# Cross attention in fp32: seven block products for two more batches, softmax sums taken by ScalarE, and the last tile's product in two column halves

## The chip, the core and the metric

The kernel runs on one core of a Trainium2 chip. The core has TensorE (matrix products, named PE in the profile, with its weight loads as PEld), VectorE (DVE), ScalarE (ACT), GpSimd (POOL) and SyncE (SP), which here issues the transfers between HBM and the on-chip memory (SBUF). TensorE writes its products into PSUM, eight banks that VectorE and ScalarE empty. Every engine works through its own queue in order, and waits at semaphores for the others. The metric is the device time of one execution in microseconds (us); less is better.

## The reference

There are 16 batches of 256 rows of x with 256 columns, and for each batch a context c of 77 rows with 192 columns. Eight heads of width 256 attend from x to c; the result is projected, added to x and normalised:

```python
Q = (x @ Wq).reshape(B, 256, 8, 256)        # and K, V from c with Wk, Wv
score = einsum('bhqd,bhkd->bhqk', Q, K) / sqrt(256)     # -inf where the mask is 0
attn = softmax(score)
out = einsum('bhqk,bhkd->bqhd', attn, V).reshape(B, 256, 2048) @ Wo + x
out = (out - mean(out)) * rsqrt(var(out) + 1e-5) * gamma + beta     # over the 256 columns
```

Everything is fp32. The output has 16 x 256 x 256 numbers.

## The kernel before

**Weights first.** For about 54 us the kernel multiplies the weights with each other: per head it forms Wq Wk^T (`gA`, `gB`) and Wv Wo (`uA`, `uB`). Afterwards the projections of x and of the output are gone: scores are x times `a`, where `a` = (Wq Wk^T) c^T, and the output is the softmax weights times `vw`, where `vw` = c (Wv Wo).

**The main loop.** It starts at line 862 and runs over batches, with b from -1 to 14. An iteration works on three batches: `new` is batch b + 1 (scores and softmax), `now` is batch b (product of the softmax weights with `vw`), `old` is batch b - 1 (layer norm and store). A batch is two tiles of 128 rows; tiles 2b and 2b + 1 belong to batch b. Each engine's instructions stand in the order in which the code issues them (`manual_schedule`), so the order of the calls is the order of the queues.

TensorE's part of an iteration: `scores` for both new tiles (line 319, into two PSUM banks for each tile), `prepare_vw` (lines 244 and 255), for b up to 10 also one quarter of `a` for the next group of four batches (`prepare_a`, lines 202 and 216), and then the product for batch b. For batches 0 to 10 (b < NS = 11) that is `seven`: the product of a batch is seen as a two by two block product, and seven block products are formed where eight would be the plain number. It needs `differences` of `vw` (`ts`, on GpSimd, line 398) and `sums` of the transposed weights (`ss`, GpSimd, lines 415 to 418), both for the next batch at the end of an iteration, and afterwards `add_seven`: ScalarE copies `m` out of PSUM (line 458), VectorE adds `po` to the rows of x (line 482), and GpSimd adds `m` (line 468, two adds in `m` and three to x). For batches 11 to 15 it is `attend` for each tile (line 384): the plain product, 256 columns wide, and one add on VectorE.

The softmax of a tile: `shift` on VectorE adds the mask from PSUM (line 334, twice) and takes the maximum (line 341); `exponential` on ScalarE, one instruction for each of eight heads (line 348); `weigh` sums each head on VectorE (line 354), takes the reciprocal (line 356) and multiplies on GpSimd (line 362, two pieces); `turn` transposes 32 by 32 blocks on VectorE (line 372) for TensorE.

The layer norm of a tile: `finish` takes statistics on VectorE (lines 490 and 493), `spread` forms the reciprocal root on ScalarE with a logarithm and an exponential (lines 502 and 503), `normalise` is either two VectorE instructions (lines 523 and 539) or, with `aside`, one on ScalarE (line 533) and two on GpSimd (lines 534 and 535), after a small scalar `less` (line 513). The stores are issued by SP, two tiles at a time (line 546), and the last two tiles one at a time (line 956).

After the loop the last batch is multiplied with `attend` for tiles 30 and 31, the layer norm of tiles 28 and 29 is done with `aside`, and those of tiles 30 and 31 follow one after the other on VectorE.

The PSUM ring has eight banks (`ps_mm`), given out in the order of the calls.

Of the kernel before, what the change touches and what calls it, by code (L numbers as in the profile page):

```python
# [8 lines left out]
F32 = mybir.dt.float32  # L9
I32 = mybir.dt.int32  # L10
AF = mybir.ActivationFunctionType
ALU = mybir.AluOpType
AX = mybir.AxisListType
PSUM = bass.MemoryType.PSUM

P = 128
H = 8
D = 256
EPS = 1e-05
GB = 4  # L20
# [33 lines left out]
def kernel(  # L54
# [53 lines left out]
    NH = DI // 2 // BK  # L108
    uA = const.tile([P, 5, NH, NF, BK], F32, tag="uA", name="uA")
    uB = const.tile([P, 5, NH, NF, BK], F32, tag="uB", name="uB")  # L110
    NS = B - GB - 1

    def of_e(u, e):
        return u[:, 3 - 2 * e : 5 - 2 * e].rearrange("p q n i c -> p (q n) i c")
# [226 lines left out]
        nc.vector.tensor_reduce(top, s, AX.X, ALU.max, negate=True)  # L341
        s_of[t] = s, top

    def exponential(t):
        e = sp.tile([P, H, S2], F32, tag="e", name=f"e_{t}")
        s, top = s_of.pop(t)
        for h in range(H):
            nc.scalar.activation(e[:, h], s[:, h], AF.Exp, bias=top[:, h : h + 1])  # L348
        e_of[t] = e

    def weigh(t):
        e = e_of.pop(t)
        den = st.tile([P, H], F32, tag="den", name=f"den_{t}")
        nc.vector.tensor_reduce(den, e, AX.X, ALU.add)  # L354
        rden = st.tile([P, H], F32, tag="rden", name=f"rden_{t}")
        nc.vector.reciprocal(rden, den)  # L356
        p = p_ring[t % 2]
        e_mh = e.rearrange("p (m h) k -> p m h k", h=2)
        rden_mh = rden.rearrange("p (m h) -> p m h", h=2)
        for cols, keys in ((slice(2 * KM), slice(KM)), (slice(2 * KM, 2 * S2), slice(KM, None))):  # L360
            part = p[:, :, cols].rearrange("p m (h k) -> p m h k", h=2)
            nc.gpsimd.tensor_tensor(  # L362
                part,
                e_mh[:, :, :, keys],
                rden_mh.unsqueeze(3).to_broadcast(list(part.shape)),
                ALU.mult,
            )
# [11 lines left out]
    def attend(t):  # L379
# [10 lines left out]
                )  # L390
        po_of[t] = po


    def differences(b):

        vw = vw_of[b].rearrange("p q k d -> p q (k d)")
        ts = vwp.tile([P, 3, 2, P], F32, tag="ts", name=f"ts_{b}", bufs=2)
        nc.gpsimd.tensor_tensor(  # L398
            ts.rearrange("p q k d -> p q (k d)"),
            vw[:, 1:4],  # L400
            vw[:, 0:1].to_broadcast([P, 3, 2 * P]),
            ALU.subtract,
        )
        ts_of[b] = ts
# [16 lines left out]
    def seven(b):  # L421
        pT = [pT_of.pop(QT * b + i) for i in range(QT)]
        vw, ss = vw_of[b], ss_of.pop(b)
        ts = ts_of.pop(b)
        pm = ps_mm.tile([P, 4, P], F32, tag="mm", name=f"pm_{b}")
        po = ps_mm.tile([P, 4, P], F32, tag="mm", name=f"po_{b}")
        t2, b21, b22, b11 = (vw[:, q] for q in range(4))
        t4, t1, t3 = (ts[:, q] for q in range(3))
        s1, s3, s2, s4 = (ss[:, i] for i in range(4))
        ends = vr[:, b, :P], vr[:, b, P:]  # L430

        def contract(out, *terms):
            for n, (weight, moving) in enumerate(terms):
                for i in range(NM):
                    nc.tensor.matmul(  # L435
                        out[i * BK : (i + 1) * BK],
                        weight[:, i],
                        moving,
                        start=(n == 0),
                        stop=(n == len(terms) - 1),  # L440
                    )

        def block(weights, moving):
            return [(weights[:, k], moving[:, k]) for k in range(2)]

        last = [(pT[i][:, NF], vr[:, b, j * P : (j + 1) * P]) for i in range(QT) for j in range(2)]
        contract(pm[:, 0], *block(pT[0][:, 0:2], b11))
        contract(pm[:, 1], *block(s2, t2))
        contract(pm[:, 2], *block(s3, t3))
        contract(pm[:, 3], *block(s1, t1))  # L450
        contract(po[:, 0], *block(pT[0][:, 2:4], b21), last[0])
        contract(po[:, 1], *block(s4, b22), last[1])
        contract(po[:, 2], *block(pT[1][:, 2:4], t4), last[2])
        contract(po[:, 3], last[3])
        for i in range(QT):
            po_of[QT * b + i] = flat(po[:, 2 * i : 2 * i + 2])
        m = vwp.tile([P, 4, P], F32, tag="m", name=f"m_{b}", bufs=1)
        nc.scalar.copy(m, pm)
        m_of[b] = m
# [24 lines left out]
    def finish(t):  # L484
        if t in po_of:
            add_product(t)
        g, j = t // GT, t % GT
        y = xg_of[g][:, j, :]
        bn = st.tile([P, 6], F32, tag="bn", name=f"bn_{t}")
        nc.vector.bn_stats(bn, y)  # L490
        if j == 0:
            mv_of[g] = st.tile([P, GT, 2], F32, tag="mv", name=f"mv_{g}", bufs=2)
        nc.vector.bn_aggr(mv_of[g][:, j, :], bn)

    all_rstd_of, rstd_of, done = {}, {}, []

    def spread(first, last):

        g, lo, hi = first // GT, first % GT, (last - 1) % GT + 1
        log = st.tile([P, GT], F32, tag="log", name=f"log_{first}")  # L500
        rstd = st.tile([P, GT], F32, tag="rstd", name=f"rstd_{first}")
        nc.scalar.activation(log[:, lo:hi], mv_of[g][:, lo:hi, 1], AF.Ln, bias=eps)
        nc.scalar.activation(rstd[:, lo:hi], log[:, lo:hi], AF.Exp, scale=-0.5)
        all_rstd_of[first, last] = rstd
# [16 lines left out]
    def centre(t):  # L521
        y = xg_of[t // GT][:, t % GT, :]
        nc.vector.scalar_tensor_tensor(
            y, y, mv_of[t // GT][:, t % GT, 0:1], gam, ALU.subtract, ALU.mult
        )
# [336 lines left out]
    for b in range(-1, B - 1):  # L862
        old = range(max(b - 1, 0) * QT, b * QT)
        now = range(max(b, 0) * QT, (b + 1) * QT)
        new = range((b + 1) * QT, (b + 2) * QT)
        for t in new:
            scores(t)
        if b == B - 2:
            for t in old:
                finish(t)  # L870
            spread(old[0], old[-1] + 1)
            invert(old[0], old[-1] + 1, aside=old)
            for t in old:
                normalise(t, aside=True)
        for t in new:
            shift(t)
        for n in range(0, 2) if b < 0 else range(b + 2, min(b + 3, B // 2)):
            turn_last(n)
        g, n = (b + 1) // GB + 1, (b + 1) % GB
        work = [prepare_vw(b + 1)]  # L880
        if g < NG:
            work.append(prepare_a(g, (n,)))
        for part_A, _, _ in work:
            part_A()
        for _, part_B, _ in work:
            part_B()
        for i, t in enumerate(new):
            exponential(t)
            if old and b < B - 2:
                finish(old[i])  # L890
            weigh(t)
        if old and b < B - 2:
            spread(old[0], old[-1] + 1)
        for _, _, copies in work:
            for dst, src in copies():
                nc.scalar.copy(dst, src)  # L896
        if b + 1 < NS:
            differences(b + 1)
        if b < NS:
            if now:  # L900
                seven(b)
            if old:
                invert(old[0], old[-1] + 1)
                normalise(old[0])
            for t in new:
                turn(t)
            if n >= NF - 2:
                for j in range((n - NF + 2) * GT // 2, (n - NF + 3) * GT // 2, 2):
                    transpose_x(g, j)
            if old:  # L910
                normalise(old[1])


            if n == NF - 1:
                load_x(g)
            elif n:
                load_xT(g, (n - 1) * GT // 2, n * GT // 2)
            if now:
                add_seven(b)
            if b + 1 < NS:  # L920
                sums(b + 1)
            continue
        for t in now:
            attend(t)
        if b < B - 2:
            invert(old[0], old[-1] + 1, aside=old[:1])
            normalise(old[0], aside=True)
            turn(new[0])
            normalise(old[1])
            turn(new[1])  # L930
            for t in now:
                add_product(t)
        else:
            turn(new[0])
            finish(now[0])
            spread(now[0], now[1])
            turn(new[1])

    for t in new:
        attend(t)
    add_product(last - 2)
    for t in (last - 3, last - 2):
        invert(t, t + 1, aside=(t,), less_on=nc.vector)
        normalise(t, aside=True)
        if t < last - 2:
            finish(t + 1)
            spread(t + 1, t + 2)
    for t in (last - 1, last):  # L950
        finish(t)
        spread(t, t + 1)
        centre(t)
        invert(t, t + 1)
        normalise(t, centred=True)
        nc.sync.dma_start(out_rows[:, t, :], xg_of[NG - 1][:, t % GT, :])


# [29 lines left out]
```

## Time and profile before

| what | value |
|---|---|
| median of 3 runs (lowest, highest) | 277.38 us (276.35, 278.02) |
| the profiled execution's own time | 276.75 us |
| its span | 274.9 us |
| TensorE busy | 267.8 us, 97% of the span |
| VectorE busy | 210.4 us, 77% |
| GpSimd busy | 160.0 us, 58% |
| ScalarE busy | 131.7 us, 48% |
| iteration with `seven` and `prepare_a` | 14.10 us |
| iteration with `attend` | 11.38 us |

The profile describes one execution. The iteration times are the distances between first `scores` products in the chain of work that ended last, for example 191.48 to 205.58 and 231.06 to 242.44. In the rows of the profile "L348 ACT ACTIVATE e<-s,top ... x16" means sixteen instructions of line 348 on ScalarE that write tile `e` from `s` and `top`. In a timeline the first number is the start in us from the beginning of the span, the second how long the row lasts, and the bracket at the end is the engine's idle time before it, with what ended it. Engines that wait for others have idle time that costs nothing in itself.

### The profile page before, as it was taken

How to read it: one execution, taken by the hardware profiler on the slowest of the kernel's cores; microseconds unless marked ns; L12 is line 12 of the kernel's file. 1: busy time of each engine (PE TensorE's matmuls, PEld its weight loads, DVE VectorE, ACT ScalarE, POOL GpSimd, SP SyncE). 2: the span in 40 equal slices, each digit the busy share in tenths (PEclk: the TensorE clock that was granted, in tenths of full speed). 3: DMA queues.
4: the chain of work that ended last, by engine and by line, in shares of the span. 5: the costliest groups of instructions: out<-in, count | busy, mean ns of one | idle time of the engine just before them, and what ended most of it. 6: DMA issues, size and time to landing. Idle time of an engine off the chain costs nothing.

```text
span 274.9 us, 13362 instructions
## 1 busy us (share of the span) xinstructions
PE 267.8 (97%) x5972; PEld 190.1 (69%) x5972; DVE 210.4 (77%) x406; ACT 131.7 (48%) x419; POOL 160.0 (58%) x221
## 2 busy tenths in 40 slices
PE   8999999999999999999999999999999999999992
PEld 7857486777494949495959585868686767585660
DVE  0364867697749898979798898878798978879875
ACT  2314112354818182837374646464555553836751
POOL 1000006919677878787878777777777537245752
PEclk9999999999999999999999999999999999999998
DMA  6995999910000132310221415101405060110112
GB/s 182 244 210 161 336 152 169 259 20 5 4 4 5 56 64 72 126 45 4 73 48 41 81 33 163 43 2 36 89 5 117 2 194 4 41 41 4 41 44 76
DMA packets 40394, 22.63 MB, mean 82 GB/s; under 512 B 23360, under 2 KB 38800, under 8 KB 40336
## 3 DMA queue, kind: packets, MB, share of 16 engines
q1 hardware_dynamic: 40336, 21.77, 32.4%
q8 instruction: 47, 0.77, 1.2%
q14 instruction: 11, 0.09, 0.1%
HBM read 17.57 MB, written 4.19 MB: 79 GB/s over the span
## 4 chain that ended last, share of the span: by engine, by line
PE 96%; DVE 2%; issue 0%; POOL 0%; POOLq 0%; DVEq 0%
PE ps L319 24%; PE pa L202 12%; PE pv L244 10%; PE po L435 9%; PE pm L435 8%; PE po L384 7%; PE pa L216 6%; PE pv L255 6%; PE pu L709 3%; PE pr L278 2%; PE idle L629 1%; PE pg L752 1%; PE pgb L709 1%; PE pw L723 1%; PE pr L290 1%; PE phb L723 1%
## 5 line engine op out<-in xcount | busy, mean ns | idle before, releaser
L348 ACT ACTIVATE e<-s,top 128x77 f32<-128x77 f32 x256 | 67.1, 347 | 68.0 <-DVE top L341 65.4
L362 POOL TENSOR_TENSOR p<-e,rden 128x512 f32<-128x512 f32 x64 | 47.2, 758 | 43.4 <-DVE rden L356 29.8
L319 PE MATMUL ps<-a,xT 128*32 128x154 f32 x2048 | 70.0, 294 | 0.0
L319 PEld LDWEIGHTS ps<-a,xT 128*32 128x32 f32 x2048 | 66.1, 110 | 1.7 <-issue 0.8
L334 DVE TENSOR_TENSOR s<-ps,bias 128x308 f32<-128x308 f32 x64 | 30.3, 474 | 17.8 <-PE ps L319 17.7
L202 PE MATMUL pa<-cA,gA 128*32 128x308 f32 x512 | 35.8, 423 | 0.0
L202 PEld LDWEIGHTS pa<-cA,gA 128*32 128x32 f32 x512 | 16.4, 110 | 20.9 <-issue 8.0
L468 POOL TENSOR_TENSOR xg<-xg,m 128x256 f32<-128x256 f32 x33 | 24.1, 732 | 11.4 <-DVE xg L482 9.7
L244 PE MATMUL pv<-uA,cA 128*32 128x512 f32 x256 | 30.4, 592 | 0.0
L354 DVE TENSOR_REDUCE den<-e 128x8 f32<-128x616 f32 x32 | 24.7, 773 | 4.4 <-ACT e L348 4.4
L372 DVE STREAM_TRANSPOSE pT<-p 128x640 f32<-128x640 f32 x32 | 25.4, 816 | 1.8 <-POOL p L362 1.8
L341 DVE TENSOR_REDUCE top<-s 128x8 f32<-128x616 f32 x32 | 25.4, 795 | 1.1
L896 ACT COPY vw<-pv 128x512 f32<-128x512 f32 x32 | 17.1, 586 | 8.9 <-PE pv L255 8.9
L539 DVE SCALAR_TENSOR_TENSOR xg<-xg,rstd,bet 128x256 f32<-128x256 f32 x25 | 19.5, 778 | 1.9
L398 POOL TENSOR_TENSOR ts<-vw 128x768 f32<-128x768 f32 x11 | 20.2, 1837 | 0.0
L216 PE MATMUL pa<-cB,gB 64*32 64x308 f32 x512 | 19.5, 420 | 0.0
L384 PE MATMUL po<-vw,pT 128*32 128x256 f32 x320 | 19.2, 380 | 0.0
L216 PEld LDWEIGHTS pa<-cB,gB 64*32 64x32 f32 x512 | 9.7, 107 | 11.3 <-issue 7.6
L255 PE MATMUL pv<-uB,cB 64*32 64x512 f32 x256 | 17.4, 601 | 0.0
L896 ACT COPY a<-pa 128x308 f32<-128x308 f32 x48 | 16.8, 457 | 0.0
L482 DVE TENSOR_TENSOR xg<-po,xg 128x256 f32<-128x256 f32 x32 | 12.1, 413 | 6.1 <-PE po L435 5.7
L384 PEld LDWEIGHTS po<-vw,pT 128*32 128x32 f32 x320 | 10.0, 110 | 9.5 <-DVE den L354 2.5
(112 smaller groups left out, 387.4 us busy)
## 6 DMA issues: line engine op xcount, KB each, us to landing
xg<-in_x_dram SPq DMA_DIRECT2D x4, 1024.0 KB, 6.9
out_dram<-xg SPq DMA_DIRECT2D x15, 256.0 KB, 2.4
xT<-in_x_dram SPq DMA_DIRECT2D x24, 128.0 KB, 3.9
wo<-in_L_xattn_Wo_dram SPq DMA_DIRECT2D x4, 512.0 KB, 5.1
wvT<-in_L_xattn_Wv_dram SPq DMA_DIRECT2D x16, 96.0 KB, 3.7
wq_nat<-in_L_xattn_Wq_dram SPq DMA_DIRECT2D x2, 512.0 KB, 6.1
wq_blk<-in_L_xattn_Wq_dram SPq DMA_DIRECT2D x8, 128.0 KB, 5.4
xT<-in_x_dram SPq DMA_DIRECT2D x4, 256.0 KB, 8.5
```

Source lines behind the costliest of these rows:

```text
L202: nc.tensor.matmul(flat(o[i * BK : (i + 1) * BK]), gA[:, h, cols(dc, i)], flat(cA[:, batches, :]), start=not B_first, stop=B_first,)
L216: nc.tensor.matmul(flat(banks[j + k][i * BK : (i + 1) * BK]), gB[half(k), h % NF, cols(dc, i)], flat(cB[half(k), batches, :]), start=B_fir ...
L244: nc.tensor.matmul(pv[k][i * BK : (i + 1) * BK], cA[:, b, k * BK : (k + 1) * BK], uA[:, parts, :, i], start=True, stop=False,)
L255: nc.tensor.matmul(pv[k][i * BK : (i + 1) * BK], cB[half(k), b, k * BK : (k + 1) * BK], uB[half(k), parts, :, i], start=False, stop=True,)
L319: nc.tensor.matmul(ps[m // 2][i * BK : (i + 1) * BK, m % 2 * 2 * S2 : (m % 2 + 1) * 2 * S2], xT_of[g][:, j * NM + m, dc], flat(a_of[g][:, ...
L334: nc.vector.tensor_tensor(s[:, a * H // 2 : (a + 1) * H // 2], ps[a][:, : H // 2 * S2].rearrange("p (h k) -> p h k", k=S2), bias[:, b, :]. ...
L341: nc.vector.tensor_reduce(top, s, AX.X, ALU.max, negate=True)
L348: nc.scalar.activation(e[:, h], s[:, h], AF.Exp, bias=top[:, h : h + 1])
L362: nc.gpsimd.tensor_tensor(part, e_mh[:, :, :, keys], rden_mh.unsqueeze(3).to_broadcast(list(part.shape)), ALU.mult,)
L384: nc.tensor.matmul(po[i * BK : (i + 1) * BK], pT[:, n, i], vw_of[b][:, 2 - n // 2 * 2 : 4 - n // 2 * 2, n % 2, :] if n < NF else vr[:, b, ...
L435: nc.tensor.matmul(out[i * BK : (i + 1) * BK], weight[:, i], moving, start=(n == 0), stop=(n == len(terms) - 1),)
L896: nc.scalar.copy(dst, src)
```

## The change

`NS` becomes 13, so batches 11 and 12 are multiplied with `seven` as well. In these two iterations (b = 11 and 12) `prepare_a` is over, and they get an order of their own for VectorE: the normalisation of the first old tile and the first `turn` come ahead of the second tile's reciprocal; both old tiles are normalised on VectorE; `spread` of the old tiles stands between the fourth and fifth exponential of the second new tile; and the differences for batch 12 are formed on VectorE. In all iterations the sums of the exponentials come from the exponentials themselves (`accum_out`), and VectorE's reduction is gone. Inside `seven` two of the four `po` products move ahead of three of the `pm` products. Tile 31 is multiplied in two halves of 128 columns, each in a PSUM bank of its own, and added and counted half by half; tile 30's layer norm is centred on VectorE, scaled on ScalarE and shifted on GpSimd.

```diff
-    NS = B - GB - 1
+    NS = B - 3
...
-    def exponential(t):
+    def exponential(t, between=None):
         e = sp.tile([P, H, S2], F32, tag="e", name=f"e_{t}")
+        den = st.tile([P, H], F32, tag="den", name=f"den_{t}")
         s, top = s_of.pop(t)
         for h in range(H):
-            nc.scalar.activation(e[:, h], s[:, h], AF.Exp, bias=top[:, h : h + 1])
-        e_of[t] = e
+            if between and h == H // 2:
+                between()
+            nc.scalar.activation(
+                e[:, h], s[:, h], AF.Exp, bias=top[:, h : h + 1], accum_out=den[:, h : h + 1]
+            )
+        e_of[t] = e, den
 
     def weigh(t):
-        e = e_of.pop(t)
-        den = st.tile([P, H], F32, tag="den", name=f"den_{t}")
-        nc.vector.tensor_reduce(den, e, AX.X, ALU.add)
+        e, den = e_of.pop(t)
         rden = st.tile([P, H], F32, tag="rden", name=f"rden_{t}")
...
+    def attend_halves(t):
+
+        b, pT = t // QT, pT_of.pop(t)
+        po_of[t] = [ps_mm.tile([P, P], F32, tag="mm", name=f"po_{t}_{c}") for c in range(2)]
+        for c, po in enumerate(po_of[t]):
+            for n in range(NF + 1):
+                for i in range(NM):
+                    nc.tensor.matmul(
+                        po[i * BK : (i + 1) * BK],
+                        pT[:, n, i],
+                        vw_of[b][:, 2 - n // 2 * 2 + c, n % 2, :]
+                        if n < NF
+                        else vr[:, b, c * P : (c + 1) * P],
+                        start=(n == 0),
+                        stop=(n == NF),
+                    )
+
-    def differences(b):
+    def differences(b, engine):
...
-        nc.gpsimd.tensor_tensor(
+        engine.tensor_tensor(
...
         contract(pm[:, 0], *block(pT[0][:, 0:2], b11))
+        contract(po[:, 0], *block(pT[0][:, 2:4], b21), last[0])
+        contract(po[:, 2], *block(pT[1][:, 2:4], t4), last[2])
         contract(pm[:, 1], *block(s2, t2))
         contract(pm[:, 2], *block(s3, t3))
         contract(pm[:, 3], *block(s1, t1))
-        contract(po[:, 0], *block(pT[0][:, 2:4], b21), last[0])
         contract(po[:, 1], *block(s4, b22), last[1])
-        contract(po[:, 2], *block(pT[1][:, 2:4], t4), last[2])
         contract(po[:, 3], last[3])
...
+    def finish_halves(t):
+        g, j = t // GT, t % GT
+        bn = st.tile([P, 2, 6], F32, tag="bn2", name="bn_halves", bufs=1)
+        for c, po in enumerate(po_of.pop(t)):
+            y = xg_of[g][:, j, c * P : (c + 1) * P]
+            nc.vector.tensor_tensor(y, po, y, ALU.add)
+            nc.vector.bn_stats(bn[:, c], y)
         nc.vector.bn_aggr(mv_of[g][:, j, :], bn)
...
-        for i, t in enumerate(new):
-            exponential(t)
+        if g < NG or b >= NS:
+            for i, t in enumerate(new):
+                exponential(t)
+                if old and b < B - 2:
+                    finish(old[i])
+                weigh(t)
             if old and b < B - 2:
-                finish(old[i])
-            weigh(t)
-        if old and b < B - 2:
-            spread(old[0], old[-1] + 1)
+                spread(old[0], old[-1] + 1)
+        else:
+            exponential(new[0])
+            finish(old[0])
+            weigh(new[0])
+            finish(old[1])
+            exponential(new[1], between=lambda: spread(old[0], old[-1] + 1))
+            invert(old[0], old[-1] + 1)
+            normalise(old[0])
+            turn(new[0])
+            weigh(new[1])
+            normalise(old[1])
         for _, _, copies in work:
             for dst, src in copies():
                 nc.scalar.copy(dst, src)
-        if b + 1 < NS:
-            differences(b + 1)
+        if g == NG and b < NS:
+            if b + 1 < NS:
+                differences(b + 1, nc.vector)
+            seven(b)
+            turn(new[1])
+            add_seven(b)
+            if b + 1 < NS:
+                sums(b + 1)
+            continue
         if b < NS:
+            differences(b + 1, nc.gpsimd)
...
-            if b + 1 < NS:
-                sums(b + 1)
+            sums(b + 1)
             continue
...
-    for t in new:
-        attend(t)
+    attend(last - 1)
+    attend_halves(last)
     add_product(last - 2)
...
-    for t in (last - 1, last):
-        finish(t)
-        spread(t, t + 1)
-        centre(t)
-        invert(t, t + 1)
-        normalise(t, centred=True)
+    def store(t):
         nc.sync.dma_start(out_rows[:, t, :], xg_of[NG - 1][:, t % GT, :])
+
+    t = last - 1
+    finish(t)
+    spread(t, last)
+    centre(t)
+    invert(t, last)
+    rstd, _ = rstd_of.pop(t)
+    y = xg_of[NG - 1][:, t % GT, :]
+    nc.scalar.activation(y, y, AF.Identity, scale=rstd)
+    nc.gpsimd.tensor_tensor(y, y, bet, ALU.add)
+    store(t)
+    finish_halves(last)
+    spread(last, NT)
+    centre(last)
+    invert(last, NT)
+    normalise(last, centred=True)
+    store(last)
```

## The prediction

> **What bounds the kernel now.** First the page: busy shares, and the chain of work that ended last.
>
> ```profile
> PE 267.8 (97%) x5972; PEld 190.1 (69%) x5972; DVE 210.4 (77%) x406; ACT 131.7 (48%) x419; POOL 160.0 (58%) x221
> ...
> PE 96%; DVE 2%; issue 0%; POOL 0%; POOLq 0%; DVEq 0%
> ```
>
> TensorE sets the time: it runs without a gap until the last tile, and only a VectorE tail follows. But VectorE is close behind. So second, the timelines of VectorE and ScalarE around one batch of the stage that changes (iteration b = 11: batch 12 is prepared, batch 11 multiplied).
>
> ```profile
> 223.24 4.20 ACT L348 ACTIVATE e<-s,top 128x77 f32<-128x77 f32 x16 [5.03 <-DVE top L341]
> 227.35 0.28 ACT L502 ACTIVATE log<-mv,eps 128x2 f32<-128x2 f32 x1
> ...
> 234.56 0.36 ACT L348 ACTIVATE e<-s,top 128x77 f32<-128x77 f32 x1 [3.22 <-DVE top L341]
> ```
>
> ```profile
> 227.47 0.80 DVE L354 TENSOR_REDUCE den<-e 128x8 f32<-128x616 f32 x1 [0.26 <-ACT e L348]
> 228.30 0.20 DVE L356 RECIPROCAL rden<-den 128x8 f32<-128x8 f32 x1
> 228.42 0.79 DVE L372 STREAM_TRANSPOSE pT<-p 128x640 f32<-128x640 f32 x1
> ...
> 230.49 0.84 DVE L372 STREAM_TRANSPOSE pT<-p 128x640 f32<-128x640 f32 x1
> 231.25 0.71 DVE L482 TENSOR_TENSOR xg<-po,xg 128x256 f32<-128x256 f32 x2
> 232.17 0.48 DVE L334 TENSOR_TENSOR s<-ps,bias 128x308 f32<-128x308 f32 x1 [0.21 <-PE ps L319]
> 233.22 0.48 DVE L334 TENSOR_TENSOR s<-ps,bias 128x308 f32<-128x308 f32 x1 [0.57 <-PE ps L319]
> 233.73 0.80 DVE L341 TENSOR_REDUCE top<-s 128x8 f32<-128x616 f32 x1
> ```
>
> The reader should see a loop: 16 exponentials on ScalarE, then VectorE's sum, reciprocal, transposes, additions, shift and maximum, then the next 16 exponentials. It goes round in 234.56 - 223.24 = 11.32 us, while VectorE waits for TensorE's scores for just 0.21 + 0.57 = 0.78 us. Whatever makes it over 0.78 us longer makes this loop the pace. Third, the end, in the chain (first line) and VectorE's timeline.
>
> ```profile
> 260.73 6.66 PE po L384 x120
> ...
> 262.77 0.79 DVE L372 STREAM_TRANSPOSE pT<-p 128x640 f32<-128x640 f32 x1
> ...
> 268.55 0.48 DVE L523 SCALAR_TENSOR_TENSOR xg<-xg,mv,gam 128x256 f32<-128x256 f32 x1
> 269.14 0.77 DVE L539 SCALAR_TENSOR_TENSOR xg<-xg,rstd,bet 128x256 f32<-128x256 f32 x1
> 269.83 0.41 DVE L482 TENSOR_TENSOR xg<-po,xg 128x256 f32<-128x256 f32 x1
> ...
> 271.54 0.48 DVE L539 SCALAR_TENSOR_TENSOR xg<-xg,rstd,bet 128x256 f32<-128x256 f32 x1
> ```
>
> The product of tile 30 needs the transpose that ends at 263.56, and starts at 260.73 + 4.45 = 265.18: 1.6 us in hand. TensorE ends at 269.50; VectorE, still busy with tile 30, takes up tile 31 0.33 us later and ends at 272.02.
>
> **What the skill says.** The Trainium skill, "ScalarE: Activation LUTs", What ACT_TABLE_LOAD costs: an ACTIVATE takes 186 ns + 0.833 N, each [128,1] pointer operand adds about 93 ns, neighbours overlap by about 93 ns. The trace agrees: for N = 77 with a bias pointer that is 344 ns, the row has 347; sixteen take 4.20 us, 262 ns each, an overlap of 85. No page prices ScalarE's accumulator output. "VectorE: DVE Perf Modes", Two Vector instructions with no wait between them, says of Vector operations that one which writes out its accumulator is two instructions, the second a read. No run here shows either yet. "SBUF — State Buffer", Who interferes with whom: a VectorE instruction with two SBUF inputs contends with a GpSimd one that reads SBUF. The trace agrees: L523 takes 0.84 us beside GpSimd's product at 229.14 and 0.48 us at 268.55.
>
> **The change part by part.** Let x be what the accumulator adds to one exponential.
>
> (1) TensorE, batches 11 and 12. `attend` for a batch is one chain piece of 4.45 us; `seven` is 1.88 + 2.18 = 4.06 us. Two batches: -0.78 us. The new order inside `seven` costs TensorE nothing; it brings `pm` later by 48 products of 28 ns (4.06/144), 1.35 us. Hidden: in the 14.1-us iterations GpSimd's adds to xg end at 208.77, the statistics read them at 211.06; its sums end at 211.78, and are needed near 216.
>
> (2) The price of x. From below: 0. If it is one more instruction of one element: 187 - 93 = 94 ns by the page, or 204 - 85 = 119 ns by the trace's `rstd` row (L503, 204 ns). With a pointer operand, 93 more: 187 to 212. I take 100 ns, so 1.6 us more ScalarE time for 16.
>
> (3) Sums leave VectorE. The first tile's sum lay beside ScalarE's work; the second's, 227.47 to 228.30, is 0.83 us of the loop.
>
> (4) Iterations up to b = 10. The tightest are those with xT transposes: at 150.29 and 151.34 VectorE waits 0.29 + 0.57 us. Slack 0.86 + 0.83 (sum gone) = 1.69 us against 1.6: it just holds, up to x = 0.106 us. The new GpSimd work of b = 10 (differences 1.84, sums 2.9) is what earlier iterations do already.
>
> (5) Iteration 11. 11.32 - 0.78 (waits for TensorE) - 0.83 (sum) + 1.60. Ln and Exp of `spread` now stand between the exponentials: + 0.42 (227.35 to 227.77). From the reciprocal to the second transpose it was 2.19 us. Now the first transpose and one normalisation go ahead, behind ScalarE; what remains is GpSimd's p (starts 0.35 later, 1.56, a hop of 0.1: 2.01) and then the differences on VectorE, 128x768: 0.15 + 768/0.96 ns, fitted to the rows L341 (616: 795 ns) and L334 (308: 474), 0.95 less 0.08 overlap. 2.88, so + 0.69. Loop: 12.42 us. GpSimd in this iteration gives up 2.0 us (L513, L534, L535 of one tile) and gains 6.1 (two adds to m of 0.5, three to xg of 0.73, four sums of 0.73): from 5.6 to 9.8 busy of 12.4, so it follows and does not lead.
>
> (6) Iteration 12, the same without differences: 11.38 - 0.83 (0.26 + 0.57 waits) - 0.83 + 0.42 + 1.60 - 0.17 = 11.57. Iteration 13 keeps the old order and has no waits for TensorE: 11.76 - 0.83 + 1.60 = 12.53. Last batch, first exponential to first transpose: 262.77 - 257.70 = 5.07 - 0.83 + 1.60 = 5.84.
>
> (7) Sum: 223.24 + 12.42 + 11.57 + 12.53 + 5.84 = 265.60; the transpose of tile 30 ends at 266.39. TensorE would want it at 265.18 - 0.78 = 264.40. **It waits 1.99 us**: both batches' gain and the hand of 1.6 us are used up.
>
> (8) The end. The column halves: 80 products of 28 ns for 40 of 56 (4.45/80): +0.04 us; both halves need the same transposed tile, so no new wait. TensorE ends at 269.50 - 0.78 + 0.04 + 1.99 = 270.75. VectorE took 6.26 us from that transpose's start to the end of centring tile 30, 0.23 of it waiting for TensorE: 265.60 + 6.03 = 271.63. Then the halves: two adds (128 columns, 0.27 by the slope from L334 to L482), two statistics (0.27), one aggregate 0.18, with gaps of 0.03 and one overlap: 1.27; logarithm and exponential 0.59; the last L539 0.48: 273.97. Before 272.02: +1.95. Tile 30's second half moving to ScalarE (0.6) and GpSimd (0.73) saves VectorE 0.77, which (8) has counted; its store is issued ahead of the last one on SP, whose wait (0.4 us an issue) is done before 273.97. If VectorE were on time, halves and move would save 0.33 + 0.29 = 0.62 us.
>
> Span 274.9 + 2.0 = 276.9; the profiled run 276.75 becomes 278.7, the median of the three runs 277.38 becomes **279.3**.
>
> **Rivals.** *A, a dear accumulator.* At x = 0.187 the four last loops add 64 x 0.087 = 5.6 us, and the six transposing iterations up to b = 10 pass their slack by 16 x 0.081 = 1.3 us each, 7.8 us that TensorE's lead cannot return: about 277.4 + 2 + 13 = 292. For it: an exponential has one pointer operand already, a read may too. Against: the page's plain price. It decides from x = 0.106. In it GpSimd's sums of batch 12, which end near 239 where TensorE wants them (its fourth block of `seven`), become a second wait.
>
> *B, the other side: a nearly free accumulator.* Each ns of x counts 64 times, so (7) and (8) break even at x = 0.100 - 1.95/64 = 0.07, and below 0.05 the loops keep up with TensorE. Then -0.78 + 0.04 - 0.62 = -1.4: 276.0. For it: the numbers of multiplications and of output elements stay the same. Against: the sum must be written somewhere, and the smallest ScalarE row is 203 ns.
>
> *C, the loops are shorter than added up*: GpSimd's p may be shorter when VectorE's order gives it the ports, or two waits overlap. Then 277 to 278. Against: L523's 0.84.
>
> **How the numbers follow.** About 0.5% (1.4 us) is what a measurement can tell from no change. My sum, x from 0.085 to 0.135, 277.8 to 283: chance 0.52, of which slower 0.39, same 0.13. A: 0.20, all slower. B: 0.18, faster 0.10, same 0.08; its floor is just at the bound. C: 0.10, same 0.06, slower 0.02, faster 0.02. Faster 0.12, same 0.27, slower 0.61. The range goes from B's floor, 276.0, up to 290, into A, whose upper part is left out.
>
> **What would show it.** Right: ScalarE's 16 exponentials take about 5.8 us instead of 4.20; first exponentials of batches 12 to 15 12.4, 11.6, 12.5 us apart; TensorE stands for 2 us before the product of tile 30, released by VectorE's transpose; chain pieces of 4.06 us twice more. Wrong: 16 in 4.3 us, and a chain that is TensorE to the last product; or waits of TensorE in every group before b = 11. The step most at risk is (2).

## The result, and the profile after

The changed kernel takes 277.8 us (median of 21 runs, 277.0 to 278.84), the kernel before on the same chip 276.72 us (median of 21, 276.0 to 278.22). The ratio is 1.0033, 95% interval 1.002 to 1.0047: about 0.9 us slower, where the prediction had 1.9.

Executions of one kernel differ by 1.5 us and more. In the traces the difference lies ahead of the main loop: from TensorE's `pc` products, which begin between 13.41 and 14.81 us, every kernel here takes 209.6 to 209.8 us to the first exponential of batch 12, and the latest of them, diff_pool, has waited until 12.3 us for the transfer of the weights `wk_last`. So inside the traces all times below are counted from that exponential, which lies between 223.04 and 224.44 us. In the kernel before, the last VectorE instruction ends 272.02 - 223.24 = 48.78 us after it, in the changed kernel 273.25 - 223.56 = 49.69: **+0.91 us**, which agrees with the ratio.

The page of the changed kernel, busy shares and chain of work that ended last:

```profile
PE 266.9 (97%) x6140; PEld 193.4 (70%) x6140; DVE 189.2 (69%) x380; ACT 152.3 (55%) x676; POOL 171.1 (62%) x235
...
PE 78%; DVE 9%; ACT 8%; DMA 2%; issue 1%; POOL 1%; SPq 0%; DVEq 0%; ACTq 0%
```

VectorE gave up 21 us of work and is less busy than before, and yet the chain, which was TensorE to 96%, now runs through ScalarE and VectorE for 17% of the span. The costliest groups (busy us, mean ns | idle before) show the accumulator:

```profile
L351 ACT ACTIVATE e<-s,top 128x77 f32<-128x77 f32 x256 | 87.9, 346 | 55.2 <-DVE top L341 55.2
...
L351 ACT ACTIVATION_READ_ACCUMULATOR e<-s,top 128x1 f32 x256 | 47.9, 187 | 0.0
...
L359 DVE RECIPROCAL rden<-den 128x8 f32<-128x8 f32 x32 | 6.3, 196 | 34.9 <-ACT e L351 34.8
```

Every exponential has a second instruction behind it, which reads the accumulator. The last row is the other side of it: VectorE's reciprocal, which before followed a sum, now waits for ScalarE, 34.8 us in all. ScalarE's timeline of iteration 11 answers the one shown of before:

```profile
223.56 0.36 ACT L351 ACTIVATE e<-s,top 128x77 f32<-128x77 f32 x1 [3.73 <-DVE top L341]
223.82 0.19 ACT L351 ACTIVATION_READ_ACCUMULATOR e<-s,top 128x1 f32 x1
223.92 0.34 ACT L351 ACTIVATE e<-s,top 128x77 f32<-128x77 f32 x1
...
227.59 0.19 ACT L351 ACTIVATION_READ_ACCUMULATOR e<-s,top 128x1 f32 x1
227.68 0.28 ACT L531 ACTIVATE log<-mv,eps 128x2 f32<-128x2 f32 x1
228.00 0.21 ACT L532 ACTIVATE rstd<-log 128x2 f32<-128x2 f32 x1
...
229.38 0.19 ACT L351 ACTIVATION_READ_ACCUMULATOR e<-s,top 128x1 f32 x1
...
235.48 0.36 ACT L351 ACTIVATE e<-s,top 128x77 f32<-128x77 f32 x1 [4.48 <-DVE top L341]
```

From start to start an exponential takes 0.343 to 0.344 us (sixteen without a break: 209.46 to 214.96), against 4.11 / 16 = 0.257 before (223.24 to 227.35). The accumulator's price x is therefore 0.086 to 0.087 us, taken as 0.086 below, though its record lasts 0.187. One turn of the loop is 235.48 - 223.56 = 11.92 us, where it was 11.32. VectorE in the same turn:

```profile
229.60 0.20 DVE L359 RECIPROCAL rden<-den 128x8 f32<-128x8 f32 x1
229.72 0.43 DVE L552 SCALAR_TENSOR_TENSOR xg<-xg,mv,gam 128x256 f32<-128x256 f32 x1
230.19 1.16 DVE L568 SCALAR_TENSOR_TENSOR xg<-xg,rstd,bet 128x256 f32<-128x256 f32 x1
231.27 1.12 DVE L418 TENSOR_TENSOR ts<-vw 128x768 f32<-128x768 f32 x1
232.31 0.83 DVE L375 STREAM_TRANSPOSE pT<-p 128x640 f32<-128x640 f32 x1
...
233.72 0.84 DVE L334 TENSOR_TENSOR s<-ps,bias 128x308 f32<-128x308 f32 x2
234.59 0.80 DVE L341 TENSOR_REDUCE top<-s 128x8 f32<-128x616 f32 x1
```

There is no bracket from the second tile's reciprocal on: VectorE waits for nothing, TensorE's scores are there when it comes. Before, it waited 0.78 us for them. TensorE and VectorE at the end (TensorE first):

```profile
264.11 0.61 PE L387 MATMUL po<-vr,pT 128*32 128x256 f32 x8
265.64 1.93 PE L387 MATMUL po<-vw,pT 128*32 128x256 f32 x32 [0.91 <-ACT vw L937]
...
269.76 0.43 PE L403 MATMUL po<-vr,pT 128*32 128x128 f32 x8
```

```profile
264.70 0.79 DVE L375 STREAM_TRANSPOSE pT<-p 128x640 f32<-128x640 f32 x1
...
270.06 0.80 DVE L552 SCALAR_TENSOR_TENSOR xg<-xg,mv,gam 128x256 f32<-128x256 f32 x1
270.78 0.28 DVE L520 TENSOR_TENSOR xg<-po,xg 128x128 f32<-128x128 f32 x1
...
272.18 0.48 DVE L552 SCALAR_TENSOR_TENSOR xg<-xg,mv,gam 128x256 f32<-128x256 f32 x1
272.77 0.48 DVE L568 SCALAR_TENSOR_TENSOR xg<-xg,rstd,bet 128x256 f32<-128x256 f32 x1
```

TensorE could have begun tile 30's product at 264.11 + 0.43 = 264.54 (0.43 is the distance at which the next product follows elsewhere), and begins at 265.64. It stands for 1.1 us, of which the profile records 0.91. VectorE reaches tile 31's first half at 270.78, after TensorE has ended at 270.19.

### The profile page after: what moved, and what is told of

The parts are those of the page before. It is cut to its first block, busy times and chain, and to the rows that moved or that the text cites. A ratio compares the mean times of both kernels' runs of the same rounds, so it can differ in the third digit from the quotient of the medians.

```text
span 276.1 us, 13922 instructions
## 1 busy us (share of the span) xinstructions
PE 266.9 (97%) x6140; PEld 193.4 (70%) x6140; DVE 189.2 (69%) x380; ACT 152.3 (55%) x676; POOL 171.1 (62%) x235
## 4 chain that ended last, share of the span: by engine, by line
PE 78%; DVE 9%; ACT 8%; DMA 2%; issue 1%; POOL 1%; SPq 0%; DVEq 0%; ACTq 0%
PE ps L319 19%; PE pa L202 12%; PE po L455 9%; PE pm L455 8%; PE pv L244 7%; ACT e L351 7%; PE pa L216 6%; PE pv L255 4%; PE pu L738 3%; PE pr L278 2%; DMA wq_nat<-in_L_xattn_Wq_dram 2%; DVE pT L375 1%; PE pg L781 1%; PE pgb L738 1%; PE pw L752 1%; DVE xg L552 1%
## 5 line engine op out<-in xcount | busy, mean ns | idle before, releaser
L351 ACT ACTIVATE e<-s,top 128x77 f32<-128x77 f32 x256 | 87.9, 346 | 55.2 <-DVE top L341 55.2
L365 POOL TENSOR_TENSOR p<-e,rden 128x512 f32<-128x512 f32 x64 | 48.4, 777 | 35.9 <-DVE rden L359 35.9
L351 ACT ACTIVATION_READ_ACCUMULATOR e<-s,top 128x1 f32 x256 | 47.9, 187 | 0.0
L488 POOL TENSOR_TENSOR xg<-xg,m 128x256 f32<-128x256 f32 x39 | 28.5, 731 | 3.2 <-DVE xg L502 0.6
L359 DVE RECIPROCAL rden<-den 128x8 f32<-128x8 f32 x32 | 6.3, 196 | 34.9 <-ACT e L351 34.8
L568 DVE SCALAR_TENSOR_TENSOR xg<-xg,rstd,bet 128x256 f32<-128x256 f32 x26 | 21.5, 827 | 2.0 <-ACT rstd L532 0.2
L418 POOL TENSOR_TENSOR ts<-vw 128x768 f32<-128x768 f32 x12 | 22.1, 1840 | 0.0
L488 POOL TENSOR_TENSOR m<-m 128x128 f32<-128x128 f32 x26 | 13.0, 499 | 12.8 <-ACT m L478 11.8
L455 PE MATMUL po<-vr,pT 128*32 128x128 f32 x416 | 18.5, 273 | 0.0
L478 ACT COPY m<-pm 128x512 f32<-128x512 f32 x13 | 7.6, 585 | 17.2 <-PE pm L455 17.2
```

The lines of the kernel that those rows point to most:

```text
L365: nc.gpsimd.tensor_tensor(part, e_mh[:, :, :, keys], rden_mh.unsqueeze(3).to_broadcast(list(part.shape)), ALU.mult,)
L455: nc.tensor.matmul(out[i * BK : (i + 1) * BK], weight[:, i], moving, start=(n == 0), stop=(n == len(terms) - 1),)
L488: nc.gpsimd.tensor_tensor(to, to, what, ALU.add)
```

## The experiments

All were timed beside the kernel before (medians 276.6 to 276.9 us). In the texts recorded before each run, "loop theory" is the prediction's account (a loop through ScalarE and VectorE paces the last batches), and a "rival" is another account with another number. "Turns" (of the loop, not the function `turn`) are the distances between first exponentials of batches 12 to 15, and from the last of these to tile 30's transpose. The two columns at the right count from batch 12's first exponential and are differences to the kernel before; 0.4% of the time is 1.1 us.

| kernel | median us | ratio (95%) | turns, us | tile 30's transpose | end |
|---|---|---|---|---|---|
| before | 276.7 | 1 | 11.32, 11.38, 11.76, 5.07 | 0 | 0 |
| changed | 277.80 | 1.0033 (1.002-1.0047) | 11.92, 11.23, 12.26, 5.73 | +1.61 | +0.91 |
| no_acc | 278.14 | 1.0053 (1.0032-1.0074) | 12.87, 11.95, 11.66, 5.08 | +2.03 | +1.34 |
| acc_only | 277.78 | 1.0037 (1.0017-1.0058) | 11.32, 11.38, 12.26, 5.72 | +1.15 | +1.04 |
| tail_only | 276.22 | 0.9986 (0.9973-0.9998) | 11.31, 11.38, 11.77, 5.07 | 0 | -0.46 |
| seven_only | 278.58 | 1.0081 (1.0051-1.0111) | 12.87, 11.94, 11.66, 5.08 | +2.02 | +1.91 |
| dose | 284.55 | 1.0276 (1.0255-1.0296) | 13.32, 12.63, 13.64, 7.12 | +7.18 | +8.16 |
| acc_odd | 277.20 | 1.0000 (0.9983-1.0017) | 12.04, 11.12, 11.52, 4.99 | +0.14 | -0.55 |
| odd_ns12 | 276.00 | 0.9974 (0.9961-0.9988) | 11.35, 10.95, 11.61, 4.99 | -0.63 | -0.85 |
| acc_late | 277.83 | 1.0043 (1.0012-1.0074) | 11.92, 11.24, 12.31, 5.73 | +1.67 | +0.99 |
| old_order | 279.83 | 1.0092 (1.0067-1.0117) | 12.63, 12.09, 12.25, 5.73 | +3.17 | +2.47 |
| diff_pool | 278.65 | 1.0061 (1.0039-1.0083) | 11.24, 12.38, 12.26, 5.73 | +2.08 | +1.38 |
| acc_ns12 | 276.94 | 0.9999 (0.998-1.0019) | 11.23, 11.08, 12.26, 5.73 | +0.77 | +0.07 |
| turn_first | 277.84 | 1.0040 (1.0026-1.0054) | 11.93, 11.23, 12.25, 4.57 | +0.45 | +0.82 |

The last column and the ratios tell the same, within 0.6 us in every row.

**The three parts, one at a time.** no_acc is the changed kernel with the sums on VectorE:

```diff
-            nc.scalar.activation(
-                e[:, h], s[:, h], AF.Exp, bias=top[:, h : h + 1], accum_out=den[:, h : h + 1]
-            )
+            nc.scalar.activation(e[:, h], s[:, h], AF.Exp, bias=top[:, h : h + 1])
...
+        nc.vector.tensor_reduce(den, e, AX.X, ALU.add)
```

> The changed kernel with the sums of the exponentials back on VectorE (one reduction per tile); seven, the order and the end stay. Loop theory: in the last four batches the loop of exponentials and VectorE loses 16 x 0.086 us of reading the accumulator and gets 0.83 us of sum back, and the first tile's sum (0.8) no longer finds room behind ScalarE, since the normalisation and the transpose have moved there (VectorE waits only 0.33 and 0.19 us there in the changed kernel's batch 12). VectorE itself is then the pace: about 1.4 us slower than before, 0.5 slower than the changed kernel (between 0.3 faster and 1.0 slower than it). Rival (the accumulator is the whole loss): TensorE is the bound again, 1.3 us faster than before.

acc_only is the same edit the other way round, in the kernel before.

> The kernel before with the accumulators alone. Loop theory: each loop grows by 1.38 - 0.83 = 0.55 us; up to batch 13 the 0.78 us of waiting for TensorE hide it; batches 14 and 15 are 1.1 us later together, within the 1.6 us in hand for tile 30's product, but VectorE's end is late by most of it: 0.7 us slower than before (0 to 1.1), no new wait of TensorE over 0.2 us. Rival (the accumulator is the whole loss of the change): as much slower than the kernel before as the accumulators take away, 2.2 us.

tail_only is the kernel before with the new end:

```diff
-    for t in new:
-        attend(t)
+    attend(last - 1)
+    attend_halves(last)
...
-    for t in (last - 1, last):
-        finish(t)
...
+    finish_halves(last)
```

> The kernel before with the changed end alone: column halves of tile 31, tile 30 scaled on ScalarE and shifted on GpSimd. Loop theory: from TensorE's last product to the last normalisation 1.9 us where it was 2.52, so 0.5 us faster than before. Rival (the new end is what costs): slower than before by 0.3 us or more, since the halves load each weight block twice and GpSimd's addition holds VectorE up.

seven_only is no_acc with the old end, so it has the seven products for batches 11 and 12, the new order there and the new order of the products inside `seven`, and nothing else.

> The changed kernel with the sums on VectorE and the end as before: seven for batches 11 and 12 with its order of VectorE alone. Loop theory: VectorE is the pace as in no_acc, and the end is the old one: 1.9 us slower than before, 0.5 slower than no_acc. Rival (seven gains what it saves on TensorE and only the accumulator spoils it): 0.78 us faster than before. Rival (seven saves nothing on TensorE): as before, 0.

All four ends came close to what was expected. The sevens with their order cost 1.91 us by the trace, the new end then gains 0.57 (1.91 to 1.34), the accumulators 0.43 (1.34 to 0.91). So the accumulators alone are not the loss: in the kernel before they cost 1.04 us, inside the longer iterations they help. The turns say why. In turn 11 VectorE is busy for 9.58 of 11.32 us in the kernel before and for 12.12 of 12.87 us in seven_only. It has taken over the differences (1.12 us) and the second old tile's normalisation, and single instructions take longer beside GpSimd, which goes from 4.89 to 9.07 us; how the 2.54 us divide was not tested. So in turns 11 and 12 VectorE is the full engine, and taking its sums away shortens them by 0.95 and 0.72 us; in turn 13 and the last, VectorE waits for ScalarE anyway, and the accumulators lengthen them by 0.60 and 0.65. In acc_only turns 11 and 12 do not change at all, because TensorE's scores still come last there. VectorE in acc_only:

```profile
233.47 0.48 DVE L334 TENSOR_TENSOR s<-ps,bias 128x308 f32<-128x308 f32 x1 [0.36 <-PE ps L319]
235.56 0.48 DVE L334 TENSOR_TENSOR s<-ps,bias 128x308 f32<-128x308 f32 x1 [0.40 <-PE ps L319]
```

Some of the slack is left, 0.36 us of it ahead of the first maximum. The new end gains in the kernel before (tail_only, 0.46) as well as behind the sevens (0.57).

**The slope.** dose adds one tiny ScalarE instruction to each exponential of the last four batches:

```diff
+            if t >= 24:
+                nc.scalar.copy(idle1, eps)
```

> The changed kernel with one more ScalarE instruction of one element per partition after each exponential of batches 12 to 15 (64 in all; it copies a constant to a column that nothing reads). Loop theory: the four last turns of the loop pace the kernel already, so each nanosecond that the instruction costs per exponential, read in the trace from start to start, counts 64 times. At 75 to 110 ns that is +4.8 to +7.0 us on the changed kernel, a span of 281 to 283 us, and the wait of TensorE before tile 30's product grows from 0.91 us to 5.5 to 7.5. Rival (the loop has slack that the accumulators have not used up, and the lost time sits in the end or in TensorE's order): under +2 us.

From start to start an exponential now takes 0.4355 us (223.48 less 223.04, and so on), 0.092 more. The transpose of tile 30 comes 5.57 us later than in the changed kernel: about 60 times 0.092, where 64 were expected. Sixty is what the loop asks for: VectorE's reciprocal waits for the last accumulator read of a turn, and the tiny instruction behind that read is not waited for, so that 15 of a turn's 16 count. The end is 7.25 us later, more than that, and TensorE's timeline shows where the rest comes from; below it the same engine in windows (PE busy, PEld, DVE, ACT, POOL, then the granted clock):

```profile
270.68 3.64 PE L390 MATMUL po<-vw,pT 128*32 128x256 f32 x32 [6.28 <-ACT vw L940]
274.07 1.11 PE L390 MATMUL po<-vr,pT 128*32 128x256 f32 x8
```

```profile
259.00:264.00 5.00, 5.00 (x92) 2.54 (x87) 4.71 (x12) 2.87 (x14) 3.57 (x7) 1.00 0.16 56
...
270.00:275.00 5.00, 4.32 (x44) 2.32 (x48) 3.35 (x10) 2.79 (x8) 2.81 (x5) 0.50 0.00 0
```

After 6.28 us without work the granted clock is 0.50, and the tile's product takes 4.24 us (270.68 to 274.92) where it takes 2.15.

**Where the accumulators cost.** acc_late leaves the first 24 tiles' sums on VectorE:

```diff
+            if t >= 24:
                 nc.scalar.activation(
                     e[:, h], s[:, h], AF.Exp, bias=top[:, h : h + 1], accum_out=den[:, h : h + 1]
                 )
+            else:
+                nc.scalar.activation(e[:, h], s[:, h], AF.Exp, bias=top[:, h : h + 1])
...
+        if not (t >= 24):
+            nc.vector.tensor_reduce(den, e, AX.X, ALU.add)
```

> The changed kernel with accumulators for batches 12 to 15 alone; the 24 tiles before have their sums on VectorE. Step (4) of the prediction: up to b = 10 the iterations hold with either, so nothing changes against the changed kernel: 277.8, within 0.4 us. Rival (the accumulators also cost in the iterations up to b = 10, where the scores begin): 277.0 or less.

Up to b = 10 either place of the sum is hidden: from the first scores of batch 0 to those of batch 12 TensorE takes 165.29 us in acc_late, and 165.30 in the kernel before and in the changed one. From there on the two kernels are the same, and their ends agree within 0.08 us. acc_odd has `t % 2 == 1` in the two conditions, so only a batch's second tile has accumulators.

> The changed kernel with accumulators for the second tile of each batch alone; the first tile's sum is VectorE's again. Loop theory: the first tile's sum (0.80 us) lies under the second tile's exponentials and costs nothing, and its accumulators cost 8 x 0.086 = 0.69 us of each turn; without them four turns are 2.75 us shorter, which is more than TensorE's wait of 0.91 us, so TensorE no longer waits and keeps the 0.74 us of its two batches. Against the kernel before: -0.4 (VectorE still late with tile 30) to -1.3 us (VectorE on time, end saves 0.62 more), so 275.4 to 276.3. Rival (sum on VectorE or on ScalarE makes little odds: all of one gave 278.1 and all of the other 277.8, and half of each lies between): 277.9.

This was missed in part. Turn 13 and the last are 0.74 us shorter each, as expected, but turns 11 and 12 hardly move (12.04 and 11.12 against 11.92 and 11.23), so the transpose comes 1.47 us earlier and not 2.75. VectorE in turn 11 of acc_odd:

```profile
225.53 0.76 DVE L362 TENSOR_REDUCE den<-e 128x8 f32<-128x616 f32 x1
226.33 0.20 DVE L364 RECIPROCAL rden<-den 128x8 f32<-128x8 f32 x1
226.45 0.38 DVE L515 BATCH_NORM_STATS2 bn<-xg 128x6 f32<-128x256 f32 x1
226.86 0.18 DVE L518 BATCH_NORM_AGGREGATE mv<-bn 128x2 f32<-128x6 f32 x1
226.96 1.05 DVE L557 SCALAR_TENSOR_TENSOR xg<-xg,mv,gam 128x256 f32<-128x256 f32 x1
```

The expectation put the first tile's sum under the second tile's exponentials, where VectorE stood idle before. In these two turns it no longer does: the statistics of the old tiles are there, and ScalarE's logarithm then waits 0.44 us for them (at 227.07). VectorE's and ScalarE's chains are equally long here, so that a longer one costs in full and a shorter one returns nothing. The end is 0.55 earlier than before by the trace, but the ratio (which is not simply that of the two medians) is 1.0000: its 14 runs spread from 275.73 to 277.70 us, more than the gain, and whether acc_odd gains stays open.

odd_ns12 is acc_odd with `NS = B - 4`, seven products for batch 11 alone.

> The same with seven products added for batch 11 alone; batch 12 keeps eight. Loop theory: one turn fewer in the long order, so VectorE is 1 us or so earlier at tile 30 and on time at the end, for 0.39 us of TensorE's time given back: against the kernel before -0.35 (one batch) -0.5 (end) = -0.9 us, 275.8. If the two batches' sevens are what pays (TensorE's count of products decides), it is 0.4 us slower than accumulators for the second tiles with both batches.

It is the fastest kernel of the study, 0.26% below the kernel before (0.12% to 0.39%), and its chain is TensorE again:

```profile
PE 96%; DMA 2%; DVE 1%; issue 0%; SPq 0%; DVEq 0%
```

Part of this gain is the new end, which alone gives 0.14% (tail_only; the two intervals overlap). No run has seven products for batch 11 and all sums on VectorE, so what the second tiles' accumulators give by themselves is open. acc_ns12 gives odd_ns12 accumulators for all tiles.

> Seven products for batch 11 added alone, the new end, and accumulators for both tiles of every batch (the best kernel so far has them for second tiles alone). Turns 13 and last are paced by ScalarE, each 0.69 us longer with the first tile's accumulators; so tile 30's transpose comes about 1.4 us later than in that kernel, at or just after the moment TensorE wants it, and VectorE is 1.1 to 1.4 us later at the end: 277.1 to 277.4, 0.4 to 0.7 over the kernel before. Rival (what helps there is one batch fewer, and the first tile's sum is free on either engine): 276.0.

Turn 13 and the last grow by 0.65 and 0.74 us, the end by 0.92 (1.1 to 1.4 were expected, and the median is below the forecast range), and the gain is gone. This is the clearest sign that the first tile's accumulators are paid for at the end of the kernel.

**VectorE's order.** old_order puts iterations 11 and 12 into the order of those before them; the branch of the old order is taken for all b < NS, with conditions for what has no next group:

```diff
-        if g < NG or b >= NS:
+        if True:
...
-        if g == NG and b < NS:
+        if False:
```

> The changed kernel with iterations 11 and 12 in the order of the iterations before them (logarithm after the exponentials, normalisation of both old tiles' first half ahead of both transposes, differences on GpSimd); accumulators, seven products and the new end stay. Loop theory: in these two turns VectorE has no gap left, and what decides is how much of its work stands between the last exponential and the next scores. The old order puts the second normalisation (0.9 us) and the first transpose (0.8) there and takes the differences (1.1) away; the turns become 0 to 0.8 us longer, and so do TensorE's wait and the end: 277.8 to 279.3. Rival (the new order is itself what costs): faster than the changed kernel, 277.3 or less.

The turns are 0.71 and 0.86 us longer, the end 1.56 later, at or beyond the upper edge of what was expected: the new order does shorten these turns, and without it the loss would be larger. VectorE behind the second reciprocal, in old_order:

```profile
230.65 1.56 DVE L375 STREAM_TRANSPOSE pT<-p 128x640 f32<-128x640 f32 x2
232.13 0.88 DVE L552 SCALAR_TENSOR_TENSOR xg<-xg,mv,gam 128x256 f32<-128x256 f32 x1
233.05 0.56 DVE L568 SCALAR_TENSOR_TENSOR xg<-xg,rstd,bet 128x256 f32<-128x256 f32 x1
```

diff_pool gives the differences of batch 12 back to GpSimd:

```diff
-                differences(b + 1, nc.vector)
+                differences(b + 1, nc.gpsimd)
```

> The changed kernel with the differences of batch 12 on GpSimd again. VectorE loses 1.04 us in iteration 11, GpSimd gains 1.84. If VectorE alone set that turn it would fall from 11.92 us to iteration 12's 11.23 and the end come 0.6 earlier: 277.2. Loop theory with GpSimd in it: GpSimd has 0.3 us of idle time in the changed kernel between iteration 11's additions and the weights of batch 13's first tile, so 1.84 us more make those weights 1.2 to 1.5 us late; VectorE's transpose waits for them, and iteration 12 returns more than iteration 11 gave: 278.2 to 278.6.

Both halves came as written, the total at the upper edge. Turn 11 falls to 11.24 us, turn 12 rises to 12.38, because GpSimd's weights of batch 13's first tile are late. GpSimd and then VectorE in diff_pool:

```profile
232.42 1.84 POOL L418 TENSOR_TENSOR ts<-vw 128x768 f32<-128x768 f32 x1
...
240.55 1.56 POOL L365 TENSOR_TENSOR p<-e,rden 128x512 f32<-128x512 f32 x2
```

```profile
242.15 0.84 DVE L375 STREAM_TRANSPOSE pT<-p 128x640 f32<-128x640 f32 x1 [1.27 <-POOL p L365]
```

**What TensorE's wait is worth.** In the changed kernel ScalarE's copies of `vw` for batch 15, queued behind tile 31's last exponential, end at 265.49 us, and so does the transpose of tile 30 (264.70 + 0.79). turn_first moves the transpose ahead of tile 31's reciprocal:

```diff
+                if i and b == B - 2:
+                    turn(new[0])
                 weigh(t)
...
-            turn(new[0])
             finish(now[0])
```

> The changed kernel with one move in the last batch: the transpose of tile 30 goes ahead of tile 31's reciprocal on VectorE. Its weights are ready at 263.50 us in the changed kernel's trace, so the transpose ends near 264.35 instead of 265.49. But ScalarE's copies of vw for batch 15, queued behind tile 31's last exponential, end at 265.49 too, at the same moment. If they are a second gate of equal height (as the profile's label ScalarE vw says), TensorE still starts tile 30's product 42.1 us after the first exponential of batch 12, with 0.9 us of idle time, and only VectorE's part of the end gains, 0.5 to 0.8 us: 277.0 to 277.3. If the transpose alone was the gate (as the prediction has it), the idle time is gone too.

Neither alternative held. TensorE in turn_first:

```profile
264.91 0.61 PE L387 MATMUL po<-vr,pT 128*32 128x256 f32 x8
265.87 1.98 PE L387 MATMUL po<-vw,pT 128*32 128x256 f32 x32 [0.34 <-DVE xg L502]
...
268.10 1.06 PE L403 MATMUL po<-vw,pT 128*32 128x128 f32 x32
```

and VectorE:

```profile
267.08 0.84 DVE L375 STREAM_TRANSPOSE pT<-p 128x640 f32<-128x640 f32 x1 [0.52 <-POOL p L365]
...
269.64 0.42 DVE L502 TENSOR_TENSOR xg<-po,xg 128x256 f32<-128x256 f32 x1
```

The product starts 41.51 us after batch 12's first exponential instead of 42.08: the transpose was the last gate by about 0.57 us. Then others end the wait, VectorE's addition at 265.87 by the label, and the first of the two copies of `vw` at 265.84. The end, however, is only 0.09 us earlier. TensorE has finished tile 30 at 268.10, and VectorE takes it up at 269.64; VectorE's second transpose now waits 0.52 us for tile 31's weights. So TensorE's wait is the visible sign, and VectorE's lateness behind the last exponential is what is paid. acc_only and acc_ns12 say the same: in both TensorE never waits at tile 30, and the end is still later, by 1.04 us than in the kernel before and by 0.92 than in odd_ns12.

## Why the prediction was right or wrong

The mechanism was right: the loop through ScalarE and VectorE paces the last batches, TensorE waits at tile 30, and VectorE is late at the end. The step that failed is the size of one term, (2). With 0.086 us in the place of its 0.100 the prediction's own sum gives +1.05 us; +0.91 was measured.

**Step (1), TensorE.** Right: in the chains, from the first scores of the last group to the moment tile 30's product could start it is 264.54 - 220.00 = 44.54 us, before 265.00 - 219.68 = 45.32: -0.78, as forecast. The new order inside `seven` is hidden.

**Step (2), the price of x: the term that was mis-sized.** The form was right: one more instruction, priced as one without a pointer operand. 100 ns were taken, 86 measured; sixteen exponentials take 5.50 us, and not 5.8. The Trainium skill, "ScalarE: Activation LUTs", What ACT_TABLE_LOAD costs, gives 186 ns + 0.833 N for an instruction with immediate operands, and the record of 187 ns agrees with N = 1; the overlap with its neighbour is 101 ns (187 less 86), and not the page's 93 or the 85 that were read from the trace. The 85 was a small misreading: 4.20 us holds the whole of the last exponential, and from start to start two exponentials overlap by 90 ns (347 less 257). 64 x 0.014 = 0.90 us of the 1.22 by which the four turns were overestimated is this. That x counts in every one of the last four turns is what dose shows, though only upwards: the way down was argued in rival B, and acc_odd shows that turns 11 and 12 return nothing.

**Steps (3) and (4).** Right: the second tile's sum was in the loop, and up to b = 10 everything holds (first exponentials 209.46 and 223.56, 14.10 us apart as before; acc_late).

**Step (5), iteration 11.** With x = 0.086 it would have been 12.20 us; it took 11.92. Up to the second reciprocal the sum was 6.25, with 0.086 it is 6.03, measured 6.04. Two other terms are too large. From there to the second transpose 2.88 was forecast, 2.71 measured: the differences were set behind GpSimd's weights, but they do not need them. They start at 231.27, while GpSimd works until 231.57, and only the transpose behind them waits for both. The rest of the loop was 3.29 and took 3.17. The 0.95 us for the differences themselves were 1.12, and the normalisation ahead of them took 1.16 beside GpSimd where it takes 0.48 alone (272.77); the Trainium skill, "SBUF — State Buffer", Who interferes with whom, says that such instructions contend, and the trace agrees. GpSimd was busy for 4.89 us in this turn before, not 5.6, and is for 9.33 now; that it follows and does not lead holds.

**Step (6).** With x = 0.086, 11.35, 12.31 and 5.62 us; measured 11.23, 12.26 and 5.73. Right.

**Step (7), the wait.** Right in place and kind, 1.10 us instead of 1.99. The transpose ends 1.22 us earlier than forecast, by the turns, most of it x. Two small terms go the other way: the product starts 0.15 us behind the transpose's end, and in the kernel before its start was read from the chain as 265.18, where TensorE's timeline has 265.00, so that 1.44 us were in hand there and not 1.6.

```profile
265.00 1.91 PE L384 MATMUL po<-vw,pT 128*32 128x256 f32 x32
```

What the step missed is that ScalarE's copies of `vw` stand at nearly the same height, and that the wait does not set the end.

**Step (8), the end.** The way over VectorE was right: 8.55 us from tile 30's transpose to the last instruction, 8.37 forecast. The centring of tile 30 took 0.80 us instead of 0.48; it starts 0.21 us into one of GpSimd's multiplications for tile 29 (line 563, from 269.85). The new end by itself is not the cause: in tail_only the centring takes 0.48. The stretch ahead of it was 0.19 shorter than forecast, and the one behind it 0.05 longer. The forecast that a VectorE in time would save 0.62 - 0.04 = 0.58 is near what tail_only shows, 0.46.

**The sum.** 42.36 us of turns became 41.14, the end section 0.18 longer: +1.95 became +0.91. That +1.05 and +0.91 lie so close is in part luck: the turns were 0.32 us shorter than x alone explains, and the longer end section hides half of it. Rival A (a dear accumulator) and B (nearly free) fall with x = 0.086. C had the loops shorter than added up and 277 to 278 us, and is right for 0.3 us of turn 11 by its second reason, an overlap (the differences under GpSimd's weights); its first, shorter weights, is wrong: they took 1.69 us at 229.88, where 1.56 was assumed. The likeliest case stands with x at the lower edge of its bracket, 0.085 to 0.135. That the bracket's 277.8 us is the measured median is chance: the forecast median of 279.3 less 64 x 0.015 is 278.3, and 277.8 comes out only from the profiled run's 278.7.

## What to carry to other kernels

When the engine that paces a stretch is made faster, ask first how much slack every other chain round the same loop has: here the 0.78 us that TensorE was to save met 0.78 us of slack on VectorE, and the iterations that save it put more work into VectorE's chain than that. Moving a reduction into another engine's instruction paid here only where the receiving engine was not the one being waited for; the fastest kernel gives it to the tiles whose reduction lies open (the second of each pair), and leaves it where it lies hidden. And a price that is paid 64 times is worth measuring in one small run first: here 0.014 us too much came to 0.90 us, as much as the whole measured change.

## What was not expected of the hardware

The accumulator's read is recorded with 187 ns and costs 86 from start to start. TensorE's granted clock was 0.50 after 6.28 us without work (dose) and 1.00 after 1.1 us (the changed kernel); the Trainium skill, "TensorE: Matmul & The Clock Gate", HAM oscillation — how this bites in real kernels, names gaps of more than about 3.4 us as those that count, and these two runs lie on either side of it.
